# Last half's statistics taken from PSUM, last four rounds added on VectorE and stored plainly, a fourth state buffer

## The chip, the cores and the metric

The kernel runs on one core of one Trainium2 chip. The time is that of one launch in device microseconds; the median of three runs counts. A profiled execution has a time of its own, and all views of the trace are of that execution. The core has five engines with a queue each: TensorE (products, PE and its weight loads PEld), VectorE (DVE), ScalarE (ACT), GpSimd (POOL) and SyncE (SP). SyncE and ScalarE issue plain DMAs, GpSimd those that add to what lies in memory.

## The reference

The input x is (4, 128, 64, 64). The first layer is a layer norm over channels, a 3x3 convolution per channel added to it, and attention in windows of 16x16 over 5x5 neighbours, in two branches of four heads; its result is added to x. The second layer takes the 4096 positions as tokens: a layer norm, linear causal attention, and then a recurrence, which is what matters here:

```python
Wx = jnp.einsum('bti,hi->bth', x, W)
flat = Wx.reshape(B * T, H)
mean = jnp.mean(flat, axis=0)
var = jnp.var(flat, axis=0)
Wx = ((flat - mean) * jax.lax.rsqrt(var + BN_EPS) * gamma + beta).reshape(B, T, H)
def step(yt, wx_t):
    yt = jax.nn.sigmoid(wx_t + yt @ Vt)
    return (yt, yt)
```

Mean and variance run over all tokens of all batches, so no step of the recurrence can begin before the last token's Wx is known. The states of all steps are added to the tokens and are the output.

## The kernel before, in words

The picture is cut into 16 bands (4 batches of 4), each band into two halves of 512 tokens, 32 halves in all. The main part (up to about 780 us) does layer 1 window by window and layer 2's attention half by half. The order of its work is written out by hand, in strings of step names (`START`, `SLOT`, `LAYER1`, `TAIL`); `in_order` then holds every engine except SyncE to the order in which the instructions were recorded. The last step of the last string is `product.c`: the product W x of the very last half.

`product` (L726) makes W x of one half in a PSUM bank. All halves but the last were scaled after the product, by VectorE (L734), into `wx`, the tile that keeps W x of all tokens; for the last half the input was normed first, and ScalarE copies the bank into `wx` (L731). In both cases VectorE then takes the half's statistics from `wx` (L740). `keep` (L714) has stored the tokens in the meantime: those of batches 2 and 3 into a scratch tensor `resd`, those of batches 0 and 1 straight into the output, `out_a`.

After the string, six products with zeros (`fill`, L259) keep TensorE going, and the pools of the main part are closed. What follows opens pools of its own in the same SBUF and PSUM memory, so its first users wait for the last users of what was there:

- `res` loads the tokens of batches 2 and 3 back (L913), two loads from SyncE and two from ScalarE.
- `mv`, `sc` and `shift` (L918 to L926) are mean and variance, the factor gamma / sqrt(var + eps) and the shift beta - mean * factor: VectorE, GpSimd twice, VectorE three times.
- Six zero fills of the recurrence's banks z (L958), two of one more bank (L960), and three products with mv, sc and shift (L962) follow on TensorE.

The recurrence treats the 4096 tokens of a batch as 128 segments of 32 steps, all at once: a state is 128 x 512 (4 batches of 128 segments). Ten warm-up rounds behind the first state bring each segment to its start, then 32 rounds count. In a round TensorE adds V times the last state (L1004) onto `z`, which VectorE has seeded with factor * W x + shift (L942), in three groups of columns, and ScalarE takes the sigmoid into `ys` (L1009). `ys` is a block of four steps from a pool of three buffers (`ring`, L904). For the output:

- batches 0 and 1: every four steps GpSimd issues a DMA that adds the block to what lies in `out_a` (L1016), eight in all;
- batches 2 and 3: in each step GpSimd adds `res` and the state into `ot`, eight buffers (L1022), and SyncE stores it (L1028). The add of the last step is VectorE's.

At the end VectorE compares the last state with the one that the warm-up gave (L1035, four instructions), TensorE sums the verdict (L1045), all engines read the flag `bad` (L1052) and branch (L1054); the slow path behind the branch isn't taken. SyncE waits for the outstanding plain stores there.

## Time and profile before

| | |
|---|---|
| median of 3 runs | 839.15 us (838.75 to 840.38) |
| profiled execution | 843.62 us |
| its span (first to last instruction) | 841.8 us |
| granted TensorE clock, mean | 0.981 |
| TensorE busy / VectorE / ScalarE / GpSimd | 96% / 82% / 63% / 30% of the span |
| last product of the main part (L730) | 778.82 to 780.08 us |
| first product of the recurrence (L1004) | 784.95 us |
| last state (L1009) ends | 828.4 us |
| last store issued (L1028) | 829.8 us |

A row of the chain has the start, the time and the engine, tile and line that the end hangs on; a row of the timeline start, time, engine, line, operation, tiles and sizes, and in brackets how long the engine had been idle and who ended that. A row of the waits has the waiting engine and line, who ended the wait, the total, the count and the longest, in us. Times are from the span's start.

### The profile page before, as it was taken

The page shows a single profiled execution, that of the slowest core. Times are in us where ns is not written, and L with a number is a line of the kernel's source. Part 1 is how long each engine was busy: PE and PEld are TensorE (multiplying, and loading weights), DVE is VectorE, ACT ScalarE, POOL GpSimd, SP SyncE. Part 2 cuts the span into 40 slices and gives each one's busy share as a digit, 9 for nine tenths or more (in the row PEclk, how much of TensorE's full clock was granted, in tenths as well). Part 3 has the DMA queues.
Part 4 walks back from the last instruction along what each step waited for, and adds up shares of the span by engine and source line. Part 5 has one row for each costly group of instructions (what it writes and reads, how often), then busy time and mean ns, then how long its engine had stood idle before and what let it go on. Part 6 is the DMA issues. An engine that isn't in the chain of part 4 may idle for free.

```text
span 841.8 us, 28915 instructions
## 1 busy us (share of the span) xinstructions
PE 806.6 (96%) x11803; PEld 642.3 (76%) x11805; DVE 693.2 (82%) x2127; ACT 530.8 (63%) x1026; POOL 254.2 (30%) x365
## 2 busy tenths in 40 slices
PE   6998999999999999999999999999999999988993
PEld 3766787878787878778787878787878878756792
DVE  6565989897989998998989898998999886466882
ACT  3675757676757576666767676757666665613782
POOL 2122232423233232413142323323332303121193
PEclk7999999999999999999999999999999999999997
DMA  4022141332323231414132232323141313121697
GB/s 140 18 64 70 42 113 42 79 79 66 91 68 97 57 103 36 109 42 119 40 86 75 62 87 67 96 65 98 39 108 39 92 41 95 44 56 38 209 224 174
DMA packets 81422, 68.81 MB, mean 82 GB/s; under 512 B 44800, under 2 KB 63872, under 8 KB 81280
## 3 DMA queue, kind: packets, MB, share of 16 engines
q1 hardware_dynamic: 53200, 43.47, 18.0%
q10 hardware_dynamic: 26928, 19.20, 9.2%
q0 software_dynamic: 1152, 4.19, 2.9%
q8 instruction: 95, 1.56, 0.8%
q14 instruction: 47, 0.39, 0.2%
HBM read 39.51 MB, written 17.89 MB: 68 GB/s over the span
## 4 chain that ended last, share of the span: by engine, by line
PE 86%; DVE 4%; DMA 4%; POOL 2%; ACT 1%; issue 1%; ACTq 0%; DVEq 0%; POOLq 0%; SPq 0%
PE bank L427 12%; PE bank L509 7%; PE bank L480 7%; PE bank L625 7%; PE bank L578 7%; PE bank L524 6%; PE bank L440 6%; PE bank L302 5%; PE bank L641 4%; PE z L1004 4%; PE bank L679 3%; PE bank L662 3%; PE bank L698 3%; PE bank L700 3%; PE bank L733 3%; PE bank L467 2%
## 5 line engine op out<-in xcount | busy, mean ns | idle before, releaser
L378 DVE SCALAR_TENSOR_TENSOR y<-ypad,cpe_w,y 128x512 f32<-128x512 f32 x240 | 191.7, 799 | 12.7 <-ACT y L376 7.7
L489 ACT ACTIVATE es<-bank 128x512 f32<-128x512 f32 x256 | 132.2, 604 | 32.1 <-PE bank L480 31.7
L285 POOL TENSOR_SCALAR rs<-mv 128x4 f32<-128x4 f32 (+2 forms) x100 | 25.3, 253 | 390.8 <-DVE mv L283 389.1
L552 POOL TENSOR_TENSOR oT<-o_sb,rden 128x512 f32<-128x512 f32 x64 | 83.0, 1297 | 119.1 <-DMA rden<-rd 104.2
L286 POOL TENSOR_TENSOR rs<-rs,mhalf 128x4 f32<-128x4 f32 (+2 forms) x100 | 106.0, 1060 | 8.3
L524 PEld LDWEIGHTS bank<-es,v_sb 128*32 128x32 f32 x3072 | 62.9, 110 | 39.2 <-issue 21.3
L480 PEld LDWEIGHTS bank<-q,k 32*64 32x64 f32 x4096 | 75.4, 130 | 2.7
L480 PE MATMUL bank<-q,k 32*64 32x96 f32 (+1 forms) x4096 | 77.5, 274 | 0.0
L512 ACT COPY den<-bank 128x512 f32<-128x512 f32 x64 | 37.4, 584 | 55.8 <-PE bank L509 55.3
L524 PE MATMUL bank<-es,v_sb 128*32 128x96 f32 (+1 forms) x3072 | 69.5, 237 | 1.6 <-DMA v_sb<-v_sb 1.6
L578 PEld LDWEIGHTS bank<-woT,oT 128*128 128x128 f32 x512 | 61.0, 196 | 13.2 <-POOL oT L552 9.6
L509 PE MATMUL bank<-es,ones 128*32 128x512 f32 x512 | 69.6, 605 | 0.6 <-ACT es L489 0.6
L427 PE MATMUL bank<-y2w,wqT 128*128 128x256 f32 x256 | 67.4, 386 | 2.4 <-DVE y2w L378 2.2
L625 PE MATMUL bank<-xl,awT 128*128 128x512 f32 x128 | 66.6, 607 | 0.0
L578 PE MATMUL bank<-woT,oT 128*128 128x128 f32 x512 | 62.3, 281 | 4.5 <-POOL oT L552 4.5
L427 PE MATMUL bank<-y2w,wkT 128*128 128x256 f32 x256 | 65.9, 380 | 0.0
L440 PE MATMUL bank<-wvT,y2w 128*128 128x256 f32 x256 | 65.9, 380 | 0.0
L535 DVE TENSOR_TENSOR dc<-dc,pad_c 128x32 f32<-128x32 f32 x64 | 25.5, 399 | 47.8 <-DMA dc<-den 47.7
L435 ACT COPY k<-bank 128x512 f32<-128x512 f32 x64 | 38.6, 603 | 41.2 <-PE bank L427 41.2
L627 ACT ACTIVATE low<-bank,minus 128x512 f32<-128x512 f32 x64 | 43.8, 685 | 24.5 <-PE bank L625 23.4
L427 PEld LDWEIGHTS bank<-y2w,wkT 128*128 128x128 f32 x256 | 47.3, 190 | 13.4 <-issue 7.5
L629 DVE SCALAR_TENSOR_TENSOR f<-low,bank 128x512 f32<-128x512 f32 x64 | 43.5, 680 | 16.6 <-ACT low L627 16.6
(131 smaller groups left out, 1687.9 us busy)
## 6 DMA issues: line engine op xcount, KB each, us to landing
rden<-rd SPq DMA_DIRECT2D x64, 256.0 KB
v_sb<-v_sb SPq DMA_DIRECT2D x128, 64.0 KB
factors<-factors ACTq DMA_DIRECT2D x31, 256.0 KB
xin<-in_xt SPq DMA_DIRECT2D x15, 512.0 KB
out<-rs_o ACTq DMA_DIRECT2D x16, 256.0 KB
resd<-rs_o ACTq DMA_DIRECT2D x16, 256.0 KB
out<-ot SPq DMA_DIRECT2D x32, 128.0 KB
out<-ys POOLq DMA_DIRECT2D x8, 512.0 KB, 7.4
```

The source lines that it names most:

```text
L286: nc.gpsimd.tensor_tensor(rs[:, :n], rs[:, :n], mhalf[:, :n], ALU.pow)
L378: nc.vector.scalar_tensor_tensor(y2, src, cpe_w[:, tap : tap + 1], y2, ALU.mult, ALU.add)
L427: nc.tensor.matmul(pps[:, br * WT : (br + 1) * WT], wT[:, br * P : (br + 1) * P], y2, start=True, stop=True,)
L440: nc.tensor.matmul(vps[:, e * 256 : (e + 1) * 256], y2[:, e * P : (e + 1) * P], wvT, start=True, stop=True,)
L480: nc.tensor.matmul(sps[h][half * KC : (half + 1) * KC, cols], w["k"][rows, k0 : k0 + KC], w["q"][rows, cols], start=False, stop=br == BR - ...
L489: nc.scalar.activation(es, sps[h], AF.Exp, scale=scale)
L509: nc.tensor.matmul(dps[rows], ones[:, :HD], w["es", h], start=True, stop=True)
L524: nc.tensor.matmul(ops[rows, cols], w["v"][:, n, c0 : c0 + HD], w["es", h][:, cols], start=(br, n) == pieces[0], stop=(br, n) == pieces[-1],)
L552: nc.gpsimd.tensor_tensor(oTs[n][:, :, :, wj * WS : (wj + 1) * WS], w["o"].rearrange("p (a r c) -> p a r c", a=BR, c=WS), w["rden"].rearra ...
L578: nc.tensor.matmul(yps[:, j * P : (j + 1) * P], oT[:, br, t], woT[:, br, :], start=br == 0, stop=br == BR - 1,)
L625: nc.tensor.matmul(zps, awT[:, m * P : (m + 1) * P], h.xl, start=True, stop=True)
L627: nc.scalar.activation(low, zps, AF.Exp, bias=minus)
```

## The change

Three edits in two places.

In `product`, for the last half alone, the statistics are taken from the PSUM bank. The aggregate and the two GpSimd instructions of the factor are recorded here as well, then the negated mean (into `shift`) and last the copy of the bank into `wx`, which is now VectorE's. `mv`, `sc` and `shift` move to the pool of constants. Behind it `shift` takes one instruction (shift * sc + beta) instead of two.

The last four steps (28 to 31) of batches 0 and 1: a tile `end_a` is loaded with what `out_a` holds for them, by SyncE behind `res`. VectorE adds each of the four states to it, and ScalarE stores it plainly after the last. The eighth accumulating DMA is gone. The last step's add of batches 2 and 3 becomes GpSimd's like the others.

The pool of `ys` has four buffers instead of three.

```diff
@@ product
         if h.factors is None:
             nc.tensor.matmul(wps, fwT, h.xl, start=True, stop=True)
-            nc.scalar.copy(wx[:, h.b, h.hb], wps.rearrange("p (k s) -> p s k", s=SEG))
+            nc.vector.bn_stats(stats[:, h.b * NH + h.hb, :], wps)
+            nc.vector.bn_aggr(mv, stats.rearrange("p n s -> p (n s)"))
+            nc.gpsimd.tensor_scalar(sc, mv[:, 1:2], 1e-5, 1.0, ALU.add, ALU.mult)
+            nc.gpsimd.tensor_tensor(sc, sc, mhalf[:, :1], ALU.pow)
+            nc.vector.tensor_scalar(shift, mv[:, 0:1], -1.0, None, ALU.mult)
+            nc.vector.tensor_copy(wx[:, h.b, h.hb], wps.rearrange("p (k s) -> p s k", s=SEG))
+            return
@@ after the main part
-    ring = rec.enter_context(tc.tile_pool(name="ring", bufs=3))
+    ring = rec.enter_context(tc.tile_pool(name="ring", bufs=4))
...
+    end_a = sp.tile([P, NA, RUN, HSEGS], F32, name="end_a")
...
-    mv = sp.tile([P, 2], F32, name="mv")
-    nc.vector.bn_aggr(mv, stats.rearrange("p n s -> p (n s)"))
-    sc = sp.tile([P, 1], F32, name="sc")
-    nc.gpsimd.tensor_scalar(sc, mv[:, 1:2], 1e-5, 1.0, ALU.add, ALU.mult)
-    nc.gpsimd.tensor_tensor(sc, sc, mhalf[:, :1], ALU.pow)
+    nc.sync.dma_start(
+        end_a.rearrange("p m r k -> p (m r k)"),
+        out_a[SEG // RUN - 1].rearrange("p m r k -> p (m r k)"),
+    )
     nc.vector.tensor_tensor(sc, sc, gamma, ALU.mult)
-    shift = sp.tile([P, 1], F32, name="shift")
-    nc.vector.tensor_tensor(shift, mv[:, 0:1], sc, ALU.mult)
-    nc.vector.tensor_tensor(shift, beta, shift, ALU.subtract)
+    nc.vector.scalar_tensor_tensor(shift, shift, sc, beta, ALU.mult, ALU.add)
@@ in the rounds
         if counts:
-            if s % RUN == RUN - 1:
+            if s >= SEG - RUN:
+                nc.vector.tensor_tensor(
+                    end_a[:, :, s % RUN], end_a[:, :, s % RUN], last[:, :NA], ALU.add
+                )
+            elif s % RUN == RUN - 1:
                 nc.gpsimd.dma_start(
...
+            if s == SEG - 1:
+                nc.scalar.dma_start(
+                    out_a[s // RUN].rearrange("p m r k -> p (m r k)"),
+                    end_a.rearrange("p m r k -> p (m r k)"),
+                )
...
-            (nc.vector if s == SEG - 1 else nc.gpsimd).tensor_tensor(
+            nc.gpsimd.tensor_tensor(
```

More of the change, by code (lines that the diff above doesn't have):

```diff
@@ L234, in conv_attn_hybrid @@
     wx = const.tile([P, B, NH, SEG, HSEGS], F32, name="wx")
+    mv = const.tile([P, 2], F32, name="mv")
+    sc = const.tile([P, 1], F32, name="sc")
+    shift = const.tile([P, 1], F32, name="shift")
     first = len(nc.cur_bb.bb.instructions)
```

## The prediction

> **What bounds the kernel now.** I read the page first, then the chain that ended last, then the timeline of the hand-over and of the end, and last the windows and waits of the recurrence.

> ```profile
> span 841.8 us, 28915 instructions
> PE 86%; DVE 4%; DMA 4%; POOL 2%; ACT 1%; issue 1%; ACTq 0%; DVEq 0%; POOLq 0%; SPq 0%
> out<-ys POOLq DMA_DIRECT2D x8, 512.0 KB, 7.4
> ```

> TensorE carries the span, but nothing before the last product (776 us) is touched, so its 86% is not the question. The change lies in two places: the hand-over from the tail to the recurrence (780 to 785 us) and the end (816 to 841.8 us). The chain there:

> ```profile
> 780.13 1.27 PE bank L259 x5
> 781.45 1.48 PE z L259 x6
> 782.92 0.44 PE bank L259 x2
> 783.36 1.49 PE bank L962 x6
> 784.95 0.54 PE z L1004 x2
> ...
> 816.09 8.43 DMA out<-ys
> ...
> 824.62 0.33 ACT ys L1009
> ```

> At the hand-over the zero fills of the banks, the products with mv, sc and shift (L962) and the first recurrence product (L1004) follow one another on TensorE without a gap over 0.1 us: TensorE, not the statistics, is the last to be ready. At 824.62 ScalarE's state of step 28 waited for a buffer that an accumulating store (816.09) still read. The statistics beside it, in the timeline:

> ```profile
> 780.12 0.58 ACT L731 COPY wx<-bank 128x512 f32<-128x512 f32 x1 [2.18 <-PE bank L730]
> 781.52 1.02 DVE L919 BATCH_NORM_AGGREGATE mv<-stats 128x2 f32<-128x192 f32 x1
> 782.90 0.56 POOL L922 TENSOR_TENSOR sc<-sc,mhalf 128x1 f32<-128x1 f32 x1
> 783.88 0.16 DVE L926 TENSOR_TENSOR shift<-beta,shift 128x1 f32<-128x1 f32 x1
> 784.08 1.37 ACT L984 ACTIVATE ys<-wx,shift,sc 128x176 f32<-128x176 f32 x3 [0.79 <-DVE shift L926]
> ```

> ScalarE's copy (780.12 to 780.70) ends while VectorE still works on the statistics of the half before. Now the recurrence and the end, by windows (start and length; busy time and count of TensorE's products, its weight loads, VectorE, ScalarE, GpSimd; granted clock; DMA share; GB/s), and ScalarE's one wait for a DMA there:

> ```profile
> 801.00:829.00 28.00, 26.00 (x159) 23.33 (x157) 21.31 (x39) 23.10 (x81) 24.43 (x34) 1.00 1.05 234
> 829.00:832.00 3.00, 0.23 (x2) 0.09 (x2) 2.05 (x9) 0.00 (x0) 1.15 (x2) 0.75 1.11 267
> 832.00:835.00 3.00, 0.00 (x0) 0.00 (x0) 0.00 (x0) 0.00 (x0) 0.00 (x0) 0.50 1.02 206
> ```

> ```profile
> ACT ys L1009 <- DMA out<-ys: 1.3, 1, 1.3
> ```

> and SyncE's last instructions, from what its lines at the branch and behind it did (durations in ns min/median/max, first and last start):

> ```profile
> L1054 SPq EVENT_SEMAPHORE  x8: 17/17/17, 833.4 to 837.3; - x8
> L1727 SPq EVENT_SEMAPHORE  x14: 17/28/28, 840.2 to 841.8; - x14
> ```

> The 16 DMA engines are full (1.02 to 1.11) from 801 to 835 us, six us beyond the last state (828.4). SyncE's last wait for a store ends at 837.3, its branch brings the next instruction at 840.2, and the span ends 1.6 later: 4.5 us follow the last landing. So the end is set by the DMA engines' backlog, and the 1.3 us stall of ScalarE is only a symptom of it.

> [...] granted clock 0.50 in 756 to 758 us, after 752 to 754 had 0.97 of 2.00 us busy, and again 0.50 in 776 to 778, after 0.45 of 2.00. [...] the 128x256 add took 926 ns on VectorE beside GpSimd's own adds, the 128x256 comparison (L1035) has a median of 421 ns. [...]

> **The change, part by part.**

> *Statistics from PSUM.* VectorE had 0.69 us of statistics on wx after the copy; it now takes them from the bank, at the same time and place (it was busy until 780.80 anyhow): 0. The aggregate ends at 782.5 as before. While GpSimd works (782.63 to 783.46) VectorE negates the mean (0.16, price of L926) and then does the copy that ScalarE did. VectorE's copy of a bank isn't in the trace in this form. Below: 0.58, ScalarE's copy of this very bank. Above: 1.03, VectorE's strided product L734 (median 1062 ns). I take 0.66: VectorE's 128x512 PSUM reads L664 have a median of 656 ns[...]. The copy ends at 782.54 + 0.03 + 0.16 + 0.66 = 783.4 (783.3 to 783.75). Then sc (783.50) and one instruction for shift instead of two: shift is ready at 783.85, 0.2 earlier; with the upper copy at 784.15, 0.1 later. ScalarE's first states would gain 0.2.

> But the bank belongs to a pool that closes behind it, and the recurrence's banks lie in the same memory. In the built order of the changed kernel, TensorE's first zero fill of a recurrence bank waits for the VectorE count that this copy completes; before, it waited for ScalarE's copy, done at 780.70, and started at 781.45 without loss. Behind the waiting fill on TensorE's queue stand 6 + 2 fills (1.48 + 0.44 = 1.92 us by the chain) and the 6 passes of L962. These cost 1.49 with their own waits, and 6 x 0.218 = 1.31 at the rate of the same size elsewhere (chain: four of L427 in 0.87). So L1004 comes at 783.4 + 0.05 + 1.92 + 1.31 = 786.7 instead of 784.95: **+1.7** (1.5 with the short copy, 2.1 with the long). VectorE's seeds need only the first fill and run ahead of this. ScalarE's table load and the loads of res lose ScalarE's copy ahead of them; cover: nothing needs res before the first add at 797.0.

> *Load of end_a.* 512 KB on SyncE's queue behind res. The DMA share is 0.08 in 794 to 797 us; at the 352 GB/s that the res loads reach it takes 1.5 us, in a hole. Needed at step 28. 0; if the cover were gone, the first stores would wait 1.5.

> *Last four steps on VectorE.* Four adds at 0.42 to 0.93 us, behind the last seed (ended 824.5); VectorE was idle 3.7 us there. The one add of the last step goes back to GpSimd (0.72 to 1.0), which no longer issues the last accumulating store (0.87). Only the last add and the four comparisons stand behind ScalarE's last state: the verdict moves by -1.3 (stall) + 1.7 (start) + 0.5 (last add) - 0.9 (the moved add) = about 0. TensorE's part of the exit was done at 838.4, 1.8 us ahead of SyncE: 0.

> *Plain store for the eighth accumulating one.* The accumulating queue takes 36.7% of 16 engines over 775 to 842 us: 0.367 x 66.8 / 8 = 3.06 us of all engines each. A plain 512 KB takes 1.5 us (above[...]). Work saved: 1.6. Besides, the last plain store (issued 829.8, waited for until 837.3, 7.5 us) stood behind the accumulating one (829.3); it now stands behind a shorter one that comes earlier, up to 0.8 more. I take **-2.0** (-1.0 to -2.4).

> *Four buffers.* The 1.3 us stall goes. What is late next: GpSimd's adds, which in the trace wait for slots of ot (1.9 us at 824.85) and so for the same DMA engines. Worth 0 while these are full.

> Sum: -0.2 (hidden behind TensorE, so 0) + 1.7 - 2.0 = **-0.3 us**. The span 841.8 belongs to an execution of 843.62; the median without profile is 839.15. Applied to it: **838.85**.

> **Rivals.**

> *Half clock (slower).* TensorE now idles from the end of the free fills (781.4) to 783.4[...]. In the trace, idle stretches of 1.9 us (before 753.0) and 1.6 us (before 776.1), with smaller ones beside them, were followed by half clock, and the 1.1 us of the stall (before 825.0) was not. [...] Then -0.3 + 1.7 = +1.4: 840.55, with the upper copy and the smaller gain up to 841.6.

> *DMA not full without the profiler (faster).* The profiled execution is 4.5 us longer than the median; if part of that is DMA, the end follows the last state. Then the stall counts (1.3), and the accumulating store (at least 5.9 us to landing, by its row) gives way to a plain one[...]: 1.7 - 1.3 - 2.7 = -2.3: 836.85. Against it: eight stores of 3.06 us every 3.9 us, with the others, are over 100% by their own packets.

> *The bank's wait costs nothing (faster).* If the copy ends before TensorE is through its free fills, or the shift is what TensorE waits for anyhow: -0.2 - 2.0 = -2.2: 836.95. Against it: times above.

> **How the numbers follow.** Main case 0.45 (own range 837.6 to 840.3), half clock 0.25 (0.16 of it over +1.7), DMA not full 0.21, free wait 0.09. What a measurement can tell from no change is about 0.2%, 1.7 us. Faster: 0.21 + 0.09 and the lower edge of the main case, less the weak part of these: 0.31. Slower: 0.16 + 0.03 = 0.19. Same: 0.50. Range 836.4 to 841.1: half of the faster cases lie below 836.9, so little under a tenth is left out there, and the worst of the half clock above.

> **What would show it.** Right: a VectorE copy of about 0.66 us near 782.7 to 783.4; the zero fills of z starting at once behind it; the first recurrence product 1.7 us later after the last product than before; no wait of ScalarE for a store; DMA share full to the end, and the last store landing 7.5 us or less after its issue, about 0.3 earlier by the span. Wrong: granted clock 0.5 just behind the hand-over (half clock), fills that start before the copy ends (free wait), or a DMA share well under 1 in the last 8 us (DMA not full).

## The result, and the profile after

| | before | after |
|---|---|---|
| median, runs taken together on one chip | 842.01 us (20 runs) | 842.78 us (20 runs) |
| ratio, 95% interval | | 1.0008 (0.9994 to 1.0021) |
| profiled execution / its span | 843.62 / 841.8 us | 842.21 / 840.4 us |
| end of the aggregate to first recurrence product | 2.41 us | 5.43 us |
| first recurrence product to span end | 56.89 us | 54.47 us |

The change makes no difference that can be measured: +0.7 us, between -0.5 and +1.8. (The ratios are estimated from all the single runs and need not equal the quotient of the medians.) The forecast change, -0.3 us, lies in that interval; the forecast time, 838.85 us with a range of 836.4 to 841.1, missed. The median of before, 839.15 in three runs, was 842.01 in twenty.

The profile shows what was taken and what was given. The chain that ended last, at the hand-over of the kernel after:

```profile
779.49 1.03 DVE mv L735
780.52 0.02 issue
780.55 0.15 DVE shift L738
780.70 0.61 DVE wx L739
781.31 0.05 issue
781.36 2.74 PE z L262 x6
784.10 0.71 PE bank L262 x2
784.80 1.30 PE bank L969 x6
786.11 33.83 PE z L1011 x212
...
825.58 5.69 DMA out<-ot
```

Before, this stretch of the chain was TensorE alone. Now it goes through VectorE's aggregate (L735), negated mean (L738) and copy (L739), and only then to the zero fills, 0.06 us behind the copy. The timeline adds who had waited how long:

```profile
780.62 0.68 DVE L739 COPY wx<-bank 128x512 f32<-128x512 f32 x1
781.36 2.74 PE L262 MATMUL z<-zeros 128*128 128x512 bf16 x6 [2.34 <-DVE wx L739]
785.94 1.28 PE L1011 MATMUL z<-ys,fvT 128*128 128x176 f32 x7
786.44 0.62 ACT L1016 ACTIVATE ys<-z 128x176 f32<-128x176 f32 x2 [3.15 <-PE z L1011]
```

TensorE waited 2.34 us for the copy. Then the six fills took 2.74 us, against 1.48 before. The windows say why (as in the prediction: start and end, length, busy time and count of the five engines, then the granted clock, the DMA share and GB/s):

```profile
782.00:785.00 3.00, 3.00 (x9) 1.39 (x8) 2.94 (x6) 1.29 (x3) 0.00 (x0) 0.58 1.08 358
801.00:829.00 28.00, 26.40 (x162) 23.90 (x161) 24.74 (x41) 23.80 (x83) 25.42 (x36) 1.00 1.05 236
829.00:832.00 3.00, 0.20 (x2) 0.09 (x2) 2.55 (x12) 0.00 (x0) 0.58 (x1) 1.00 1.04 283
832.00:835.00 3.00, 0.00 (x0) 0.00 (x0) 0.00 (x0) 0.00 (x0) 0.00 (x0) 0.55 0.70 261
```

The granted clock behind the hand-over is 0.58: half clock from 781.1 to 784.5. At the end the DMA engines are busy 0.70 of the last of these windows, where they were at 1.02 before, and move more (261 GB/s against 206): the backlog ends sooner. The accumulating stores on the page, and SyncE at its last wait and behind the branch:

```profile
out<-ys POOLq DMA_DIRECT2D x7, 512.0 KB, 7.7
```

```profile
L1070 SPq EVENT_SEMAPHORE  x8: 17/17/17, 835.1 to 835.8; - x8
L1743 SPq EVENT_SEMAPHORE  x14: 17/28/28, 838.8 to 840.4; - x14
```

Seven instead of eight. SyncE's last wait ends at 835.8 and the span 4.6 later, the same distance as before (4.5). So in these two executions the start lost 3.0 us (5.43 against 2.41) and what follows gained 2.4 (54.47 against 56.89). Not all of these 2.4 us come from the new end, as the experiments show.

### The profile page after: what moved, and what is told of

The parts are those of the page before. It is cut to its first block, busy times and chain, and to the rows that moved or that the text cites. A ratio compares the mean times of both kernels' runs of the same rounds, so it can differ in the third digit from the quotient of the medians.

```text
span 840.4 us, 28917 instructions
## 1 busy us (share of the span) xinstructions
PE 804.8 (96%) x11803; PEld 641.5 (76%) x11805; DVE 696.9 (83%) x2131; ACT 530.5 (63%) x1025; POOL 255.8 (30%) x365
## 4 chain that ended last, share of the span: by engine, by line
PE 84%; DVE 6%; DMA 4%; POOL 2%; ACT 1%; issue 1%; ACTq 0%; SPq 0%; POOLq 0%; DVEq 0%
PE bank L430 12%; PE bank L483 7%; PE bank L581 7%; PE bank L512 7%; PE bank L628 7%; PE bank L527 6%; PE bank L443 6%; PE bank L305 5%; PE z L1011 4%; PE bank L644 4%; PE bank L682 3%; PE bank L665 3%; PE bank L701 3%; PE bank L703 3%; PE bank L742 3%; PE bank L470 2%
## 5 line engine op out<-in xcount | busy, mean ns | idle before, releaser
L538 DVE TENSOR_TENSOR dc<-dc,pad_c 128x32 f32<-128x32 f32 x64 | 23.2, 363 | 48.9 <-DMA dc<-den 48.9
## 6 DMA issues: line engine op xcount, KB each, us to landing
xin<-in_xt SPq DMA_DIRECT2D x15, 512.0 KB
out<-ys POOLq DMA_DIRECT2D x7, 512.0 KB, 7.7
```

## The experiments

Whole times of this kernel spread by over 1% from run to run (834.75 to 846.7 us for before), so each kernel's profile was read by stages too. The stages up to the last state are far steadier: kernels with the same start and the new end agree there to 0.05 us where no half clock comes in. The stretch behind the last state is not: it differs by more than 1 us between profiles of kernels with the same end. All values are us from one profile each; "last state" is the end of ScalarE's last sigmoid; "half clock" is a stretch of granted clock 0.5 between 740 us and the recurrence, with its start and length. What each kernel is stands below the table.

| kernel | aggregate's end to first product | aggregate's end to last state | first product to span end | aggregate's end to span end | half clock |
|---|---|---|---|---|---|
| before | 2.41 | 45.87 | 56.89 | 59.30 | 755.4 (3.4), 775.9 (3.4) |
| before_again | 2.41 | 45.13 | 55.84 | 58.25 | 755.1 (3.4) |
| e_stats | 3.89 | 46.54 | 57.63 | 61.52 | none |
| e_stats_b | 3.90 | 46.02 | 55.31 | 59.21 | 753.3 (3.4) |
| e_end | 2.41 | 44.94 | 55.14 | 57.55 | 756.2 (3.4), 776.7 (3.4) |
| e_bufs | 2.41 | 44.92 | 55.70 | 58.11 | none |
| e_end_bufs | 2.41 | 44.89 | 54.91 | 57.32 | none |
| after | 5.43 | 47.23 | 54.47 | 59.90 | 753.8 (3.4), 781.1 (3.4) |
| after_again | 3.90 | 45.70 | 54.49 | 58.39 | none |
| after_third | 3.90 | 45.69 | 54.45 | 58.35 | 753.6 (6.8), 777.5 (3.4) |
| e_fills | 3.90 | 45.66 | 55.87 | 59.77 | none |
| e_nofills | 6.77 | 48.57 | 55.57 | 62.34 | 753.9 (3.4), 781.2 (6.8) |
| e_nofills_b | 5.47 | 47.27 | 54.32 | 59.79 | 752.1 (3.4), 772.6 (3.4), 779.4 (3.4) |
| e_copy_first | 2.26 | 44.53 | 54.86 | 57.12 | 752.8 (6.8), 776.7 (3.4) |
| e_act_copy | 2.23 | 44.80 | 54.27 | 56.50 | none |
| act_again | 2.23 | 44.80 | 54.33 | 56.56 | none |
| e_warm | 2.23 | 44.80 | 54.72 | 56.95 | none |
| e_drop | 2.23 | 44.79 | 53.26 | 55.49 | 756.5 (3.4), 777.0 (3.4) |

### The three edits one by one

**The first edit alone** (e_stats, and its second profile e_stats_b); three buffers and eight accumulating stores as before:

```diff
-            nc.scalar.copy(wx[:, h.b, h.hb], wps.rearrange("p (k s) -> p s k", s=SEG))
+            nc.vector.bn_stats(stats[:, h.b * NH + h.hb, :], wps)
+            nc.vector.bn_aggr(mv, stats.rearrange("p n s -> p (n s)"))
...
+            nc.vector.tensor_copy(wx[:, h.b, h.hb], wps.rearrange("p (k s) -> p s k", s=SEG))
+            return
...
+    nc.vector.scalar_tensor_tensor(shift, shift, sc, beta, ALU.mult, ALU.add)
```

> The kernel before with the first edit alone: the last half's statistics, the aggregate and VectorE's copy taken from the PSUM bank. Theory (the wait for the bank): the zero fills of z start within 0.1 us behind VectorE's copy, with 2 to 2.5 us of wait, and the first recurrence product comes 1.7 us later after the last product than before (4.9 us there), 3.0 to 3.4 if the fills run at half clock, as in the profile of the changed kernel; the end is as before (first recurrence product to span end 56.9 us). Time +1.5 to +3.2 us, ratio 1.002 to 1.004. Rival (the bank's wait costs nothing, the start is hidden by the DMA engines' backlog at the end): the first product comes later, but the last store lands no later after the last product, and the time is within 0.5 us of before.

Measured: 841.57 us median of 14 runs, ratio to before 1.0005 (0.9988 to 1.0022). Its timeline:

```profile
781.43 0.68 DVE L739 COPY wx<-bank 128x512 f32<-128x512 f32 x1
782.16 1.48 PE L262 MATMUL z<-zeros 128*128 128x512 bf16 x6 [2.35 <-DVE wx L739]
785.22 3.95 PE L1006 MATMUL z<-ys,fvT 128*128 128x176 f32 x24
```

The wait is there (2.35 us, until the copy), the fills run at full clock (1.48), and the first product comes 3.89 us behind the aggregate, 1.48 later than before. So the wait and what is queued behind it cost 1.5 us at this place, without half clock. The whole time is too coarse to confirm or exclude that: the interval reaches from -1.0 to +1.9 us, and most of the forecast +1.5 to +3.2 lies outside it.

> The first edit alone, a second profile: aggregate's end to first recurrence product 3.9 us, or 5.4 with half clock there; first recurrence product to span end 55.8 to 57.7 us, as in the kernel before, since the end is not changed.

Measured: 3.90 us, no half clock at the hand-over; first product to span end 55.31, a little below the range. Two profiles of the same kernel differ here by 2.3 us (57.63 and 55.31): the end with eight accumulating stores is not steady. Nor is the end with seven: behind the last state it takes 12.4 us in e_end_bufs and 14.1 in e_fills.

**The second edit alone** (e_end):

```diff
+    end_a = sp.tile([P, NA, RUN, HSEGS], F32, name="end_a")
...
+            if s >= SEG - RUN:
+                nc.vector.tensor_tensor(
+                    end_a[:, :, s % RUN], end_a[:, :, s % RUN], last[:, :NA], ALU.add
+                )
...
+            if s == SEG - 1:
+                nc.scalar.dma_start(
...
-            (nc.vector if s == SEG - 1 else nc.gpsimd).tensor_tensor(
+            nc.gpsimd.tensor_tensor(
```

> The kernel before with the second edit alone: the tile for the last four steps of batches 0 and 1, VectorE's four adds, the plain store; three buffers of states. Theory (DMA engines full): first recurrence product to span end falls by 1.0 to 2.4 us from 56.9, the time by the same (ratio 0.997 to 0.999), the start is unchanged. Rival (DMA engines not full, the end follows the last state): the stall of ScalarE at step 28 of 1.3 us stays and the accumulating store's longer landing goes, -2.7 us. Rival for no gain: VectorE's adds beside GpSimd's hold up the last store, 0 to -0.5 us.

Measured: 840.07 us, 22 runs, ratio 0.9982 (0.9967 to 0.9998), so -1.5 us (-2.8 to -0.2). First product to span end 55.14: 1.0 below the mean of the three profiles with the old end and the same start (56.89, 55.84, 55.70: 56.14). The forecast of -1.0 to -2.4 agrees. By the time alone neither rival is out: -2.7 lies at one edge of the interval and -0.2 to -0.5, the case that VectorE's adds hold up the last store, at the other. In this profile ScalarE had no wait for a store although there are three buffers.

**The third edit alone** (e_bufs):

```diff
-    ring = rec.enter_context(tc.tile_pool(name="ring", bufs=3))
+    ring = rec.enter_context(tc.tile_pool(name="ring", bufs=4))
```

> The kernel before with the third edit alone: four buffers of states instead of three. Theory (DMA engines full): ScalarE's 1.3 us wait for the accumulating store goes, the last state ends 1.3 us earlier, and the last landing doesn't move: 0 (within 0.4 us). Rival (the end follows the last state): -1.3 us, ratio 0.9985.

Measured: 839.81 us, 22 runs, ratio 0.9991 (0.9975 to 1.0007): neither excluded. First product to span end 55.70, within what the old end gives with three buffers (55.31 to 57.63). What the edit is worth inside the change is shown by the pair e_end (55.14) and e_end_bufs (54.91), which differ by 0.2 us, no more than single profiles of one kernel do; their last states come alike (44.94, 44.89). And the stall that it removes does not come in every execution. ScalarE's waits in the second profile of before:

```profile
ACT ys L1009 <- DMA out<-ys: 0.6, 1, 0.6
```

It was 1.3 us in the first profile, 0.6 here, and absent in e_stats_b, which has the same three buffers; in e_stats a wait of 0.67 us stands at that step (824.07), which the trace puts down to TensorE.

**The kernel before once more** (before_again), with no edit:

> The kernel before once more, for a second profile. Theory (the stages are steady, the spread of the times comes from half-clock stretches whose place shifts between executions): aggregate's end to first recurrence product 2.4 us, first recurrence product to span end 56.4 to 57.4 us, stall of ScalarE at the last block within 1.0 to 1.6 us; half clock at other places than in the first profile. Rival (the spread comes from the end, where the DMA engines' service differs): first recurrence product to span end off by over 1 us.

Measured: one time, 842.44 us; 2.41 us and 55.84. The stage at the hand-over repeats to 0.01 us. What follows is off by 1.05, so the rival is right that some of the spread lies there: 0.74 of it comes before the last state (45.87 against 45.13), where the stall was 1.3 us and now 0.6, and 0.31 behind it. The half-clock stretches before 740 us differed as well (20.5 us in all in this execution, 13.7 in the first).

### The wait at the hand-over

**ScalarE's copy put back into the changed kernel** (e_act_copy; again as act_again):

```diff
+            nc.scalar.copy(wx[:, h.b, h.hb], wps.rearrange("p (k s) -> p s k", s=SEG))
             nc.vector.bn_stats(stats[:, h.b * NH + h.hb, :], wps)
...
-            nc.vector.tensor_copy(wx[:, h.b, h.hb], wps.rearrange("p (k s) -> p s k", s=SEG))
```

> The changed kernel with one thing put back: ScalarE copies the bank into wx as before, right behind the product, and VectorE's copy is gone. Theory (the bank's wait costs 1.7 us at the start, 3.0 with half clock): the zero fills of z no longer wait, the first recurrence product comes 4.7 to 5.0 us after the last product's start to end as in the kernel before, granted clock 1.0 behind the hand-over, and the time is 1.7 to 3 us under the changed kernel, 2.0 to 2.4 under the kernel before (ratio 0.997 to 0.998). Rival (the start is hidden by the DMA engines' backlog): the same time as the changed kernel, within 0.5 us of it.

Measured: 838.63 us, 22 runs, ratio 0.9972 (0.9955 to 0.9989). On the same chip it was 2.6 us under the first edit alone (means of the runs; 1.2 to 4.1), from which it differs in the end too. The timeline of its second profile:

```profile
777.15 0.59 ACT L734 COPY wx<-bank 128x512 f32<-128x512 f32 x1 [1.22 <-PE bank L733]
778.92 1.48 PE L262 MATMUL z<-zeros 128*128 128x512 bf16 x6 [0.50 <-DVE stats L735]
782.15 7.08 PE L1011 MATMUL z<-ys,fvT 128*128 128x176 f32 x40
```

The fills wait 0.50 us for the statistics, the new last reader of the bank, and are through long before the shift: the first product comes 2.23 us behind the aggregate, the earliest of all. The wait of the change was for VectorE's copy and nothing else. Of the 1.67 us between the two kernels at the first product (3.90, 2.23) almost half is back by the last state: it comes 45.70 us behind the aggregate's end in the changed kernel at full clock and 44.80 here. Part of that is regained in the first round (the end of its last sigmoid is at 5.27 and 4.19), most likely because ScalarE's first states and VectorE's seeds lie ready where TensorE comes late; the rest is regained late, behind round 20 (25.07 and 23.89). At the span's end the distance is 1.8 again (58.39, 56.56); what lengthens the changed kernel's end behind its last state (12.7 us, 11.8 here) stays open.

> The changed kernel with ScalarE's copy of the bank, once more. Theory: aggregate's end to first recurrence product 2.2 to 2.3 us, first recurrence product to span end 54.3 to 54.9; 1.5 to 3.0 us under the changed kernel, 1.5 to 2.5 under before (ratio 0.997 to 0.998). Rival (the first measurement of it was luck of the half-clock stretches): within 0.7 us of the changed kernel.

Measured: 840.99 us, 14 runs, ratio 1.0005 (0.9988 to 1.0021), and no different from the changed kernel beside it (841.12). The stages came out as expected (2.23; 54.33), the whole time did not: here the rival's case came, and in one of two measurements the 2 us do not show. This is the only set in which the two kernels ran side by side, so a gain of the whole time by ScalarE's copy is not shown. Its runs had a mean granted clock of 0.9833 there and 0.9855 the first time, which is one stretch of 3.4 us at half clock more (0.5 x 3.41 / 840 = 0.002); why that chip or hour had more of them is open.

**VectorE's copy ahead of its statistics** (e_copy_first), in the changed kernel:

```diff
+            nc.vector.tensor_copy(wx[:, h.b, h.hb], wps.rearrange("p (k s) -> p s k", s=SEG))
             nc.vector.bn_stats(stats[:, h.b * NH + h.hb, :], wps)
...
-            nc.vector.tensor_copy(wx[:, h.b, h.hb], wps.rearrange("p (k s) -> p s k", s=SEG))
```

> The changed kernel with VectorE's copy of the bank put ahead of its statistics. Theory (TensorE waits for the last reader of the bank): the last reader is now the statistics, done before TensorE is through its free fills, so no wait of TensorE; the aggregate comes 0.6 to 0.7 us later after the last product, and the first recurrence product follows the aggregate's end by 2.2 to 2.4 us: 0.6 to 0.7 us later after the last product than in the kernel before. Time 1.5 to 2.0 us under before (ratio 0.9976 to 0.9982). Rival (the chain of the statistics doesn't matter, only its place in VectorE's queue): the first product as late as in the changed kernel.

Measured: 839.87 us, 14 runs, ratio 1.0006 (0.9988 to 1.0024).

```profile
782.26 1.02 DVE L736 BATCH_NORM_AGGREGATE mv<-stats 128x2 f32<-128x192 f32 x1
782.29 1.48 PE L262 MATMUL z<-zeros 128*128 128x512 bf16 x6 [0.38 <-DVE stats L735]
785.54 3.71 PE L1011 MATMUL z<-ys,fvT 128*128 128x176 f32 x19
```

The fills start beside the aggregate, not behind the copy, and the first product comes 2.26 us behind the aggregate, so the order in VectorE's queue is what made them wait; the rival is out. The whole time does not follow: the forecast 1.5 to 2.0 us under before lie outside the interval, which reaches from -1.0 to +2.0. This profile had three stretches of half clock behind 740 us; whether that holds for the other runs is not known, but their mean granted clock was 0.9826, the lowest of the five kernels measured in that set. The delay of the aggregate could not be read: the last product fell into half clock in this execution, so that VectorE was idle when it came.

### Does the wait draw half clock?

**The changed kernel twice more** (after_again, after_third), with no edit:

> The changed kernel once more, for a second profile and more times. Theory (the wait draws half clock, as in the first profile): again half clock just behind the hand-over, aggregate's end to first recurrence product 5.4 us, time 0 to 1.5 us over before (ratio 1.000 to 1.002). Rival ([...] as in the kernel with the first edit alone, which had none): 3.9 us, granted clock 1.0 there, the time between 1.0 us under and 0.7 over before, depending on how many executions draw it.

Measured: 841.12 us, 14 runs, ratio 1.0003 (0.9984 to 1.0022); 3.90 us, clock 1.00 from 779 to 785. The rival, in this execution.

> The changed kernel, a third profile: aggregate's end to first recurrence product 5.4 us with half clock there, or 3.9 without; first recurrence product to span end 54.3 to 54.9 us in both.

Measured: 843.41 us in one run; 3.90 and 54.45. One of three profiles of the changed kernel, and none of two of the first edit alone, had half clock behind the hand-over.

**More fills, and none** (e_fills and e_nofills), in the changed kernel:

```diff
-    fill(bank(), 6)
+    fill(bank(), 16)
```

That is e_fills; e_nofills takes the line away and puts none in its place.

> The changed kernel with 16 instead of 6 products with zeros in the last bank of the main part, ten more of 0.21 us each, which lie in TensorE's 2.3 us of wait for VectorE's copy. Theory (part of the loss is half clock that the idle TensorE draws, in some executions): the wait stays, the z fills still start behind the copy, the granted clock is 1.0 from 779 to 786 us, aggregate's end to first recurrence product 3.7 to 4.1 us (5.4 in the profile of the changed kernel), the time 0.5 to 1.5 us under the changed kernel. Rival (half clock there comes from the idle stretches before 776 us, not from this wait): as the changed kernel, within 0.5 us, half clock still found there.

Measured: 840.69 us, 14 runs, ratio 1.0004 (0.9981 to 1.0026).

```profile
781.12 1.48 PE L262 MATMUL z<-zeros 128*128 128x512 bf16 x6 [0.17 <-DVE wx L739]
```

Only 0.17 us of idle time is left, the clock is full, and the first product still comes 3.90 behind the aggregate: the 1.5 us at the first product are the wait itself. (From there to the span's end it took 55.87, 1.4 more than in the changed kernel; the last state comes alike, 45.66, so this is the unsteady end.) That it had no half clock tells little, since two of three profiles without the added fills had none either.

> The changed kernel without the six products with zeros in the main part's last bank, so that TensorE idles from the last product's end until VectorE's copy is done, some 3.6 us instead of 2.3. Theory (the idle time in the wait draws half clock): half clock just behind the hand-over, aggregate's end to first recurrence product 5 to 5.5 us instead of 3.9, the time 0.5 to 1.5 us over the changed kernel (ratio to before 1.001 to 1.003). Rival (half clock there has another cause): 3.9 us, granted clock 1.0 there, the time of the changed kernel (1.000 to 1.001).

Measured: 841.71 us, 14 runs, ratio 1.0006 (0.9984 to 1.0027). Windows and timeline of its profile:

```profile
782.00:785.00 3.00, 2.88 (x7) 1.04 (x8) 2.62 (x8) 1.46 (x4) 0.21 (x1) 0.50 1.05 363
785.00:788.00 3.00, 3.00 (x8) 2.36 (x7) 1.14 (x3) 0.00 (x0) 0.00 (x0) 0.50 1.09 345
```

```profile
782.12 2.74 PE L262 MATMUL z<-zeros 128*128 128x512 bf16 x6 [3.65 <-DVE wx L739]
788.05 1.29 PE L1010 MATMUL z<-ys,fvT 128*128 128x176 f32 x7
```

Half clock came for two stretches (781.2 to 788.0), and the first product is 6.77 us behind the aggregate, more than the forecast 5 to 5.5. The time leaves both cases open.

> The same kernel without the six fills, a second profile: as in the first, half clock behind the hand-over (theory), or none (rival).

Measured: 840.21 us in one run; half clock from 779.4 to 782.8, 5.47 us. Both profiles with 3.0 to 3.65 us of idle time drew it, against one of five with 1.6 to 2.4 us. So half clock does follow idle time in this wait: without the fills it came in both profiles, and at the 2.3 us of the change in one of three. When it comes, one stretch costs 1.5 us, at the first product (5.43 against 3.90) and still at the last state (47.23 against 45.70).

### The end

**First edit undone** (e_end_bufs), in the changed kernel:

```diff
-            nc.vector.bn_stats(stats[:, h.b * NH + h.hb, :], wps)
...
-            return
+            nc.scalar.copy(wx[:, h.b, h.hb], wps.rearrange("p (k s) -> p s k", s=SEG))
...
+    nc.vector.bn_aggr(mv, stats.rearrange("p n s -> p (n s)"))
```

> The changed kernel with the first edit undone: the product, ScalarE's copy and the statistics as before; the plain store of the last four steps and four buffers of states stay. Theory (the end gains, the start loses): aggregate's end to first recurrence product 2.4 us as before, first recurrence product to span end 54.3 to 54.5 us (before 56.9), the time 2.0 to 2.6 us under before (ratio 0.997 to 0.9976) and about as short as the changed kernel with ScalarE's copy. Rival (statistics from PSUM are themselves worth something when ScalarE copies): this kernel 0.2 to 0.7 us slower than that one.

Measured: 839.42 us, 22 runs, ratio 0.9991 (0.9975 to 1.0008); 2.41 and 54.91 us. The 54.91 are a little over the forecast 54.3 to 54.5, and the 2.0 us of whole time lie at the edge of the interval (-2.1 to +0.7). From the aggregate on 57.32 us, 1.5 below the mean of the two profiles of before (58.78). The kernel with ScalarE's copy is 0.8 shorter than this one (56.5). Of that, 0.2 is the shorter shift at the first product (2.23 against 2.41) and 0.1 is left at the last state; the rest lies in the unsteady end.

This kernel is the change without the wait, so it also prices the wait. The changed kernel at full clock is 1.49 us behind it at the first product, 1.06 at the end of the fifth round and of the twentieth, 0.8 at the last state (45.70, 44.89) and 1.05 at the span's end (58.37, 57.32).

**No store of the last block** (e_drop): the four added states of batches 0 and 1 never leave the core, so their output is incomplete; the rest is e_act_copy.

```diff
-            if s == SEG - 1:
-                nc.scalar.dma_start(
-                    out_a[s // RUN].rearrange("p m r k -> p (m r k)"),
-                    end_a.rearrange("p m r k -> p (m r k)"),
-                )
```

> The changed kernel with ScalarE's copy of the bank, and without the store of the last four steps of batches 0 and 1: their output lacks the states. Theory (the DMA engines' backlog sets the end): 512 KB less at the end, 1.0 to 2.0 us shorter than with the store. Rival (the last state and the last small store's own landing set the end): 0 to 0.5 us shorter.

Measured: 837.24 us, 22 runs, ratio 0.9963 (0.9946 to 0.9980); 2.0 us under e_end_bufs on the same chip, from which it differs at the start too (57.32 against 55.49 behind the aggregate). First product to span end 53.26, 1.04 below the two profiles of the kernel with the store (54.27, 54.33). So the plain store costs about 1.0 us at the end, by one profile. The accumulating one is 1.1 to 2.0 dearer (next section), which makes it 2 to 3 us.

### A version with less half clock

**Fills in two idle stretches of the tail** (e_warm): e_act_copy with

```diff
-    "output.c measure.c norm.a spread.z keep.z turn.a norm.c turn.c",
+    "output.c measure.c norm.a spread.z keep.z warm.8 turn.a norm.c turn.c",
...
-    "turn_last.c product.z product.c",
+    "warm.7 turn_last.c product.z product.c",
```

> The changed kernel with ScalarE's copy of the bank, and with eight products with zeros in TensorE's idle stretch before the last half pair's transposes (1.8 us, ahead of turn.a) and seven in the one before the last half's (1.6 us, ahead of turn_last.c). Theory (half clock in the tail, one or two stretches of 3.4 us in some executions, comes from these two idle stretches and makes most of the spread): no half clock between 740 and 790 us, the time 0.5 to 2.5 us under the same kernel without them, and less spread. Rival (half clock there has other causes, or the added products delay the transposes): the same time or up to 0.5 us slower.

Measured: 839.03 us, 22 runs, ratio to before 0.9991 (0.9976 to 1.0005). On the same chip it was 1.8 us under the same kernel without these fills (ratio of means 0.9978, 0.9964 to 0.9993) and 2.1 under the changed kernel (0.9974, 0.9960 to 0.9989), with a mean granted clock of 0.9866 against 0.9833 and 0.9835. It beats the changed kernel; that it beats before is likely by the stages and not shown by the times. The spread did not shrink (standard deviation 1.8 us against 1.9).

## Why the prediction was right or wrong

- **"TensorE, not the statistics, is the last to be ready."** Only in part. In the kernel before, the weight load ahead of the first recurrence product waited for ScalarE's first states, and these for the shift (L984 in the prediction's timeline):

```profile
783.71 0.30 PEld L962 LDWEIGHTS bank<-sc,ident 128*128 128x128 f32 x2 [0.32 <-DVE sc L923]
784.91 0.30 PEld L1004 LDWEIGHTS z<-ys,fvT 128*128 128x128 f32 x2 [0.47 <-ACT ys L984]
```

  So the shorter shift is hidden behind TensorE only where the bank's wait is longer. Where that wait is gone, 0.18 us of it show (2.23 against 2.41).
- **Statistics from PSUM: 0, the aggregate as before.** Right. The aggregate ends 2.80 us behind the last product's end in the kernel after, 2.86 in the second profile of before. (2.46 in the first, where that product itself ran late in half clock.)
- **VectorE's copy 0.66 us.** Right: 0.68.
- **The bank's wait moves the first product by +1.7.** Right in mechanism, and 0.2 too large at that place: +1.49 at full clock. The forecast then put all of it into the whole time, and that is not so: 1.06 us are left in the rounds, 0.8 at the last state and 1.05 at the span's end, against the same kernel without the wait (e_end_bufs). From the aggregate's end the forecast had 4.16 us (786.7 - 782.54), the runs 3.90. The negated mean and the copy overlapped with what is ahead of them (fills start 0.84 behind the aggregate, not 0.91), and from the first fill to the first product it was 3.06 instead of 3.23. The copy by ScalarE, which takes the wait away, brings 1.67 us back here (3.90 to 2.23). (With the short copy of 0.58 us the prediction's own sum gives 1.65, not 1.5.)
- **Load of end_a 0.** No stage shows it. It wasn't tried alone.
- **Four adds on VectorE 0.** The durations were wrong; what they cost was not isolated. See the last section.
- **Plain store -2.0.** Right in direction, and -2.0 is the upper end of what the runs give; the range's lower end, -1.0, was the author's estimate. The three profiles of the changed kernel have 54.47 us on average from first product to span end and the two of the first edit alone 56.47: -2.0. But e_fills and e_nofills, with the same end, took 55.87 and 55.57. Among kernels without the wait, e_end and e_end_bufs have 55.03 on average and those with the old end (before twice, e_bufs) 56.14: -1.1. The whole time of the new end alone gives -1.5 (-2.8 to -0.2). Comparing the changed kernel with before (54.47 and 56.37) mixes in the 0.7 us that a late first product regains by the last state. Of the split, the plain store cost about 1.0, not 1.5; the accumulating one lies between 2 and 3, where the forecast had 3.06. The "up to 0.8 more" for the order is not seen.
- **Four buffers 0.** Right in the sum (0.2, within the spread), but the reason that the runs support is another one: with the last accumulating store gone, no profile shows ScalarE waiting for a store, with three buffers or four. The reading that full DMA engines make the stall worth nothing was loose. In stretches of 3 us with a share over 1 the packets of the traces add up to 559 KB (e_end_bufs, 804 to 807 us) as well as to 1,125 KB (e_act_copy, 825 to 828); in these traces a share over 1 does not mark a fixed rate that was used up.
- **Half clock rival.** It happened in one of three profiles of the changed kernel; +1.7 was forecast, half of a stretch of 3.4 us as the profile of before has two (755.4 and 775.9 us), and 1.5 measured. Its chance, 0.25, is not contradicted by that; three profiles can't confirm it.
- **DMA not full without the profiler: -2.3; the bank's wait costs nothing: -2.2.** Neither. The first would have had the end gain 4.0 us (1.3 + 2.7) with the new end and four buffers, and e_end_bufs took 0.8 us off the time (at most 2.1) and 1.5 off the stage. Its hint, that the profiled execution was 4.5 us longer than the median, was the spread of single executions: the profiled one of the changed kernel, of e_act_copy and of act_again lie below their medians (836.29 against 838.63 in e_act_copy), those of e_stats and e_nofills above. Its 2.7 us for a plain store in place of the accumulating one were the author's estimate and were not shown: the traces here give no time to landing for the plain store. The second falls by the 1.5 us that the first product came later in every full-clock profile with the wait.
- **The sum.** From the aggregate's end to the span's end: 58.78 us before (59.30, 58.25), 58.37 after at full clock (58.39, 58.35), 59.90 with half clock. That is -0.4 and +1.1, where the forecast had -0.3 and +1.4. That the first agrees so well is partly luck: by e_end_bufs (57.32) it is made of -1.5 for the end and +1.05 for the wait, where the forecast had -2.0 and +1.7, so two terms that were too large offset each other. One in three of the latter makes about +0.1 as a mean, inside what the runs gave (+0.7, -0.5 to +1.8; +0.3, -1.3 to +1.8).
- **"Applied to it: 838.85": the step that failed.** The change was applied to a median of three runs that lay within 1.6 us of one another, as if the kernel's time were known to that. These three are among the twenty of the result, where they rank first, second and sixth from below. The median of before was 842.01, 841.29, 840.28, 840.05 and 841.4 in sets of 19 to 67 runs, and single runs went from 834.75 to 846.7. The range, built from cases of the change alone, had no room for it: with the base of the measurement, 842.01, the same sum gives 841.7, and the measured 842.78 lies 1.1 above it, which the interval of the measured change (-0.5 to +1.8, with -0.3 in it) covers. So of the 3.9 us by which 838.85 was off, 2.9 are the base. (The half-clock rival's worst case, given as 841.6, comes to 841.95 by its own terms.)

Where does that spread come from? Each run has a mean granted clock. Over 67 runs of before in one set, time and clock go together with a correlation of -0.82, and 0.002 less clock, which is one stretch of 3.41 us at half rate, goes with 1.2 us more. In the profiles, too, the end of the last product of the main part, ahead of which only e_warm changes anything, moves from 775.2 us (10 us of half clock before it) to 781.3 us (27 us). That is a correlation; the nearest to a test of it is e_warm, with less half clock and 1.8 us less time.

## What to carry to other kernels

Ask of an operation that moves to another engine not only who reads its output, but who waits for it to let go of its input: here an early copy off the path became the last reader of a closing pool, and eight free fills had to queue behind it. Compare small changes by stages between fixed marks of the trace, up to a mark that repeats (the last state does here, the span's end does not), and follow a delay to the last mark before you put it into a sum. Give an absolute time the spread of the base it stands on. Look at a short wait of TensorE with the clock in mind: here the same wait of 2.3 us cost 1.5 us at the first product in two profiles of the changed kernel (3.90 against 2.41) and 3.0 in the third (5.43), where the granted clock was 0.5 behind it.

## What the runs showed of the hardware that was not expected

**A VectorE add beside GpSimd's adds took 3.1 us.** Timeline of the kernel after, the adds into end_a and GpSimd's into ot:

```profile
825.06 3.31 POOL L1038 TENSOR_TENSOR ot<-res,ys 128x256 f32<-128x256 f32 x4
825.57 4.29 DVE L1023 TENSOR_TENSOR end_a<-end_a,ys 128x256 f32<-128x256 f32 x3 [0.26 <-ACT ys L1016]
```

and the group of these adds in that stretch (the two figures behind the bar are the busy time in us and the mean in ns):

```profile
L1023 DVE TENSOR_TENSOR end_a<-end_a,ys 128x256 f32<-128x256 f32 x4 | 4.7, 1215 | 0.3 <-ACT ys L1016 0.3
```

The forecast had 0.42 to 0.93 us each. One of the three in the second row lasts from 825.57 to 828.67, just past the end of GpSimd's four in a row (828.37). In after_again it was 3.54 us (824.09 to 827.63) behind four, in e_act_copy 2.75 behind three, in e_nofills 4.15 behind five; each time it ends 0.3 us behind GpSimd's last add of the row. It does not always come so: in e_end_bufs no add took more than 0.94. So the add lasted for the rest of the row, not for one of GpSimd's adds (0.83 us in the kernel after: four in 3.31). The records fit VectorE not getting its turn between GpSimd's instructions; no run tests that. The last block's store was issued 2.2 us behind the last state in the kernel after (827.74, 829.90), and that of the last ot 1.4 behind it in the kernel before (828.41, 829.78). Whether the 0.8 us are worth anything at the end was not tried.

**Statistics from PSUM cost here what they cost from SBUF**: 0.68 us for 128x512 from the bank, 0.69 from wx (L734 and L749 of the kernel after). VectorE's copy of the bank, which reads it in strides of 32 elements (L739), took 0.68 as well.
